# Attention in steps by graph: early masks, one block of weighted sums per graph, keys for two graphs at a time

## The chip, the cores and the metric

The kernel runs on one core of one Trainium2 chip. The metric is device time in microseconds (us), from the first to the last instruction of the core; lower is better. Executions of one kernel agree within 0.3%. A ratio of two kernels is the mean time of one kernel's fast runs over that of the other's of the same rounds on the same chip, so not quite the ratio of the medians that are quoted beside it.

Terms: TensorE does the matrix products and writes them to PSUM, a small memory from which another engine has to copy a result out ("evict" it) before its buffer can be filled again. In profile lines PE is TensorE, PEld its weight loads, DVE VectorE, ACT ScalarE and POOL GpSimd; L191 is line 191 of that run's kernel. The granted clock is the share of full speed at which TensorE was clocked, 1 or 0.5 in these records. A round is the work on four graphs; a run of sums is an unbroken series of weighted sums on TensorE.

## The reference, cut to what matters

128 graphs of 128 nodes with 256 features go through two layers. The first is a graph attention with a feed-forward; the second is an attention in which each of four relations has its own values:

```python
q, k = heads(src @ Wq + bq), heads(src @ Wk + bk)       # 8 heads of 32
attn = softmax(q @ k.T / sqrt(32))
out = 0
for r in range(4):
    v_r = heads(src @ Wv[r] + bv[r])
    out = out + (attn * (adj == r)) @ v_r
x = layernorm(src + out @ Wo + bo)
x = layernorm(x + gelu(x @ W1 + b1) @ W2 + b2)
# cut: the first layer (two graph attentions, layer normalisation, feed-forward)
```

All is float32.

## The kernel before

Four graphs make a group. In each round of the program four stages run on four groups at once: the graph attention (`gat_block`) of one, the first feed-forward (`ff0`) of the one before, the relational attention of the one before that, and the last feed-forward (`ff1`). Each stage is a generator; `together` emits their steps side by side. What is emitted first has priority, and an instruction that is ready may be placed ahead of one that is not, so each engine's fixed order comes from both. The kernel has eight buffers in PSUM: four "mm", two "tr" (transposes), two "av" (weighted sums).

```python
def attention(h, at):
    hT = transposed(h)                 # PE, copies: c=0 by ScalarE, c=1 by VectorE
    for c in range(DC):                # two halves of four heads
        p = mm(wq, hT)
        nc.vector.tensor_scalar(qT[:, c], p, bq.., SCALE, op0=OP.add, op1=OP.mult)
        p = mm(wkk, hT)                # keys of all four graphs
        for q in range(HC):
            nc.scalar.activation(kbd[c][rows, :, q], p[rows], AF.Identity, bias=bk..)
        yield
    ...
    for b in range(G):
        v = values(b)                  # 8 matmuls, evicted by VectorE
        for c in range(DC):
            e = weights(b, c)          # scores, exponential (ScalarE), scaling (GpSimd)
            if pending: by_relation(*pending)   # the half before
            pending = (b, c, e, v, oT)
            yield
    by_relation(*pending)
    layernorm(y, "11")

def by_relation(b, c, e, v, oT):
    # 4 transposes of e into pT, then
    for r in range(R):
        m = wk.tile([P, HC, N], F32, name="m", bufs=4)
        nc.vector.scalar_tensor_tensor(m, ab, r, pT, op0=OP.is_equal, op1=OP.mult)
        for q in range(HC):            # weighted sums on 32 columns of the array
            nc.tensor.matmul(po[ts(q, DH)], v[...], m[:, q], tile_position=(0, q * DH), ...)
    ...                                # copy oT; for the second half: output matmul, add to y

def layernorm(y, k):
    # VectorE: statistics, rstd = var + eps;  GpSimd: rstd ** -0.5
    # VectorE: y = (y - mean) * rstd;         GpSimd: y * gain, y + offset
```

## Time and profile before

| | |
|---|---|
| time, median of 3 | 4056.95 us (4056.15 to 4057.38) |
| TensorE / VectorE / ScalarE / GpSimd busy | 94 / 48 / 35 / 32% |
| mean granted clock of TensorE | 0.975 |
| TensorE idle (span less busy) | 4055.9 - 3807.5 = 248 us |
| TensorE's wait for masks | 82.8 us |
| runs of weighted sums, one relation each mostly | 819 |

The engine that sets the end is TensorE. Its busy share alone is not enough: a change of tile is counted as busy, and a half-speed clock makes busy time longer. So three terms are looked at in all that follows: idle time, time lost to a slow clock (span times one less the mean clock; 4055.9 x 0.025 = 101 us here), and runs of sums. The first two overlap: by the clock records of the trace, 26 of the 101 us fall while TensorE is idle anyway.

### The profile page before, as it was taken

How to read it: one execution, taken by the hardware profiler on the slowest of the kernel's cores; microseconds unless marked ns; L12 is line 12 of the kernel's file. 1: busy time of each engine (PE TensorE's matmuls, PEld its weight loads, DVE VectorE, ACT ScalarE, POOL GpSimd, SP SyncE). 2: the span in 40 equal slices, each digit the busy share in tenths (PEclk: the TensorE clock that was granted, in tenths of full speed). 3: DMA queues.
4: the chain of work that ended last, by engine and by line, in shares of the span. 5: the costliest groups of instructions: out<-in, count | busy, mean ns of one | idle time of the engine just before them, and what ended most of it. 6: DMA issues, size and time to landing. Idle time of an engine off the chain costs nothing.

```text
span 4055.9 us, 50631 instructions
## 1 busy us (share of the span) xinstructions
PE 3807.5 (94%) x19984; PEld 2190.8 (54%) x19984; DVE 1959.5 (48%) x4292; ACT 1439.2 (35%) x4124; POOL 1287.7 (32%) x808
## 2 busy tenths in 40 slices
PE   5799999999999999999999999999999999999997
PEld 4455555555555555555555555555555555555554
DVE  2454554554554544545544545445555455455453
ACT  1233433333333333333333333333343343333332
POOL 1332332333323323323323233233233233233332
PEclk8999999999999999999999999999999999999998
DMA  4000000000000000000000000000000000000000
GB/s 154 6 9 19 19 4 16 19 19 19 19 3 16 19 19 19 3 16 19 19 19 19 4 16 19 19 19 9 14 16 19 19 19 3 11 9 6 6 6 11
DMA packets 28877, 70.75 MB, mean 17 GB/s; under 512 B 5600, under 2 KB 11616, under 8 KB 28640
## 3 DMA queue, kind: packets, MB, share of 16 engines
q1 hardware_dynamic: 21328, 63.19, 4.5%
q10 hardware_dynamic: 7312, 4.34, 0.4%
q8 instruction: 157, 2.57, 0.3%
q14 instruction: 80, 0.66, 0.1%
HBM read 50.74 MB, written 16.78 MB: 17 GB/s over the span
## 4 chain that ended last, share of the span: by engine, by line
PE 75%; POOL 13%; DVE 7%; ACT 1%; issue 1%; DMA 0%; POOLq 0%; DVEq 0%; ACTq 0%
PE mm L201 23%; PE mm L191 18%; PE av L310 8%; PE mm L280 8%; PE mm L288 5%; DVE tok L176 4%; POOL tok L178 3%; POOL tok L179 3%; POOL tok L186 3%; POOL rstd L174 3%; PE tr L303 2%; PE mm L316 2%; PE tr L158 2%; PE mm L263 2%; PE mm L242 1%; PE mm L251 1%
## 5 line engine op out<-in xcount | busy, mean ns | idle before, releaser
L296 POOL TENSOR_TENSOR e<-e,s 128x512 f32<-128x512 f32 x256 | 266.1, 1039 | 1820.9 <-DVE s L295 1691.4
L294 ACT ACTIVATE e<-mm,nm 128x128 f32<-128x128 f32 x1024 | 361.8, 365 | 862.4 <-DVE nm L290 861.3
L308 DVE SCALAR_TENSOR_TENSOR m<-at,tr 128x512 f32<-128x512 int32 x1024 | 645.7, 678 | 4.9 <-PE tr L303 4.9
L191 PE MATMUL mm<-T,w 128*128 128x512 f32 x1024 | 548.4, 651 | 12.5 <-DVE T L160 12.5
L201 PE MATMUL mm<-w,fT 128*128 128x256 f32 x2048 | 515.5, 390 | 0.0
L191 PE MATMUL mm<-T,wf 128*128 128x512 f32 x1024 | 465.1, 602 | 51.8 <-ACT T L162 44.1
L201 PE MATMUL mm<-wf,fT 128*128 128x256 f32 x2048 | 494.9, 387 | 0.0
L310 PE MATMUL av<-m,v 128*32 128x128 f32 x8192 | 414.5, 294 | 85.0 <-DVE m L308 82.8
L280 PE MATMUL mm<-wv,T 128*128 128x512 f32 x1024 | 464.1, 595 | 2.9 <-DVE v L281 2.1
L310 PEld LDWEIGHTS av<-m,v 128*32 128x32 f32 x8192 | 178.7, 112 | 467.9 <-DVE m L308 252.7
L281 DVE TENSOR_TENSOR v<-mm,bv 128x512 f32<-128x512 f32 x256 | 175.7, 687 | 528.8 <-PE mm L280 527.3
L201 PEld LDWEIGHTS mm<-w,fT 128*128 128x128 f32 x2048 | 368.8, 190 | 83.6 <-issue 43.5
L201 PEld LDWEIGHTS mm<-wf,fT 128*128 128x128 f32 x2048 | 373.6, 190 | 74.5 <-issue 25.4
L202 DVE TENSOR_TENSOR tok<-tok,mm 128x512 f32<-128x512 f32 x128 | 88.0, 687 | 655.5 <-PE mm L201 645.0
L178 POOL TENSOR_TENSOR tok<-tok,lng 128x1024 f32<-128x1024 f32 x128 | 300.8, 2350 | 190.2 <-DVE tok L176 190.2
L191 PEld LDWEIGHTS mm<-T,wf 128*128 128x128 f32 x1024 | 188.3, 191 | 273.3 <-issue 178.8
L176 DVE TENSOR_SCALAR tok<-tok,mv,rstd 128x256 f32<-128x256 f32 x512 | 187.0, 430 | 292.4 <-POOL rstd L174 292.4
L280 PEld LDWEIGHTS mm<-wv,T 128*128 128x128 f32 x1024 | 194.8, 191 | 234.9 <-issue 220.3
L179 POOL TENSOR_TENSOR tok<-tok,lnb 128x1024 f32<-128x1024 f32 x128 | 300.8, 2350 | 7.5
L290 DVE TENSOR_REDUCE nm<-mm 128x4 f32<-128x512 f32 x256 | 176.8, 691 | 224.3 <-PE mm L288 224.2
L193 ACT ACTIVATE fT<-mm,b 128x512 f32<-128x512 f32 x256 | 175.9, 687 | 285.1 <-PE mm L191 283.8
L191 PEld LDWEIGHTS mm<-T,w 128*128 128x128 f32 x1024 | 183.0, 199 | 166.3 <-issue 139.6
(65 smaller groups left out, 4402.7 us busy)
## 6 DMA issues: line engine op xcount, KB each, us to landing
xt<-in_xT_dram SPq DMA_DIRECT2D x32, 512.0 KB, 4.4
tok<-in_x_dram SPq DMA_DIRECT2D x32, 512.0 KB, 3.7
out_dram<-tok SPq DMA_DIRECT2D x32, 512.0 KB, 2.6
at<-in_adjT_dram SPq DMA_DIRECT2D x32, 256.0 KB, 2.7
wf<-in_wf_dram SPq DMA_DIRECT2D x2, 1024.0 KB, 9.6
w<-in_w_dram SPq DMA_DIRECT2D x2, 1024.0 KB, 9.6
wv<-in_wv_dram ACTq DMA_DIRECT2D x2, 512.0 KB, 9.9
lng<-in_g_dram ACTq DMA_DIRECT2D x4, 128.0 KB, 6.0
```

Source lines behind the costliest of these rows:

```text
L176: nc.vector.tensor_scalar(y[:, b], y[:, b], mv[:, b, 0:1], rstd[:, b:b + 1], op0=OP.subtract, op1=OP.mult)
L178: nc.gpsimd.tensor_mul(y, y, over_graphs(ln[k][0]))
L179: nc.gpsimd.tensor_add(y, y, over_graphs(ln[k][1]))
L191: nc.tensor.matmul(p, win[:, c, ts(f, P)], hT[:, c], start=c == 0, stop=c == DC - 1)
L201: nc.tensor.matmul(p[:, b - b2_], fT[f][:, ts(b, N)], wout[:, f], start=f == 0, stop=f == FC - 1)
L280: nc.tensor.matmul(p, hT[:, f, ts(b, N)], wv[:, f, r:r + 2], start=f == 0, stop=f == DC - 1)
L288: nc.tensor.matmul(p, qT[:, c, ts(b, N)], kbd[c][:, b], start=True, stop=True)
L290: nc.vector.tensor_reduce(nm, p, AX.X, OP.max, negate=True)
L294: nc.scalar.activation(e[:, q], p[:, q], AF.Exp, bias=nm[:, q:q + 1], accum_out=s[:, q:q + 1])
L296: nc.gpsimd.tensor_mul(e, e, per_row(s, N))
L308: nc.vector.scalar_tensor_tensor(m, ab, r, pT, op0=OP.is_equal, op1=OP.mult)
L310: nc.tensor.matmul(po[ts(q, DH)], v[:, r, c * P + q * DH:c * P + (q + 1) * DH], m[:, q], start=r == 0, stop=r == R - 1, tile_position=(0, ...
```

## The change

The intent: fewer changes of tile, by making all eight masks of a graph first and then all 64 weighted sums in one block; and masks that are ready long before. To make room for eight masks, keys are kept for two graphs, not four.

```diff
+    KG = G // 2
-    kbd = [cst.tile([P, G, HC, N], F32, name=f"kbd{c}") for c in range(DC)]
+    kbd = [cst.tile([P, KG, HC, N], F32, name=f"kbd{c}") for c in range(DC)]
     def attention(h, at):
         hT = transposed(h)
+        yield
         for c in range(DC):
             # cut: the query matmul and its eviction by VectorE stay
-            # cut: keys of four graphs, half c
-            yield
+        def keys(b0):           # cut: keys of graphs b0, b0 + 1, both halves
+        def weights(b):         # cut: both halves; e1 bufs 3 -> 4
+        def by_relation(b, es): # cut: 8 transposes, 8 masks; m bufs 4 -> 8
+        def weighted(ms, v):    # cut: 32 calls = 64 matmuls, one copy of oT
+        keys(0)
+        yield
+        es = weights(0)
+        yield
+        for b in range(G):
+            ms = by_relation(b, es)
+            v = values(b)
+            yield
+            if b + 1 < G:
+                if (b + 1) % KG == 0:
+                    keys(b + 1)
+                es = weights(b + 1)
+                yield
+            oT = weighted(ms, v)
+            yield
+            # cut: output matmul, add to y
         layernorm(y, "11")
-            (attention(...), 10, 0.0, 1.0)
+            (attention(...), 15, 0.0, 1.0)
```

More of the change, by code (lines that the diff above doesn't have):

```diff
@@ L264, in attention @@
             nc.vector.tensor_scalar(qT[:, c], p, bq[:, c:c + 1], SCALE, op0=OP.add, op1=OP.mult)
-            p = ps.tile([P, G, N], F32, name="mm")
-            for f in range(DC):
-                nc.tensor.matmul(p, wkk[:, f, ts(c, P)], hT[:, f], start=f == 0, stop=f == DC - 1)
-            for q in range(HC):
-                rows = ts(q, DH)
-                nc.scalar.activation(kbd[c][rows, :, q], p[rows], AF.Identity, bias=bk[rows, c:c + 1])
-            yield
         y = h
         nc.gpsimd.tensor_add(y, h, over_graphs(bo))
+        def keys(b0):
+            for c in range(DC):
+                p = ps.tile([P, KG, N], F32, name="mm")
+                for f in range(DC):
+                    nc.tensor.matmul(p, wkk[:, f, ts(c, P)], hT[:, f, b0 * N:(b0 + KG) * N],
+                                     start=f == 0, stop=f == DC - 1)
+                for q in range(HC):
+                    rows = ts(q, DH)
+                    nc.scalar.activation(kbd[c][rows, :, q], p[rows], AF.Identity, bias=bk[rows, c:c + 1])
@@ new lines, in weights @@
+        def weights(b):
+            es = []
+            for c in range(DC):
+                p = ps.tile([P, HC, N], F32, name="mm")
+                nc.tensor.matmul(p, qT[:, c, ts(b, N)], kbd[c][:, b % KG], start=True, stop=True)
+                nm = sm.tile([P, HC], F32, name="nm1")
+                nc.vector.tensor_reduce(nm, p, AX.X, OP.max, negate=True)
+                s = sm.tile([P, HC], F32, name="s1")
+                e = wk.tile([P, HC, N], F32, name="e1", bufs=4)
+                for q in range(HC):
+                    nc.scalar.activation(e[:, q], p[:, q], AF.Exp, bias=nm[:, q:q + 1], accum_out=s[:, q:q + 1])
+                nc.vector.reciprocal(s, s)
+                nc.gpsimd.tensor_mul(e, e, per_row(s, N))
+                es.append(e)
+            return es
@@ new lines, in by_relation @@
+        def by_relation(b, es):
+            ab = at[:, b][:, None, :].to_broadcast([P, HC, N])
+            ms = []
+            for e in es:
+                pT = ps.tile([P, HC, N], F32, name="tr", bufs=2)
+                for q in range(HC):
+                    nc.tensor.transpose(pT[:, q], e[:, q], ident)
+                ms.append([])
+                for r in range(R):
+                    m = wk.tile([P, HC, N], F32, name="m", bufs=DC * R)
+                    nc.vector.scalar_tensor_tensor(m, ab, r, pT, op0=OP.is_equal, op1=OP.mult)
+                    ms[-1].append(m)
+            return ms
@@ L283, in values @@
             return v
-        def weights(b, c):
-            p = ps.tile([P, HC, N], F32, name="mm")
-            nc.tensor.matmul(p, qT[:, c, ts(b, N)], kbd[c][:, b], start=True, stop=True)
-            nm = sm.tile([P, HC], F32, name="nm1")
-            nc.vector.tensor_reduce(nm, p, AX.X, OP.max, negate=True)
-            s = sm.tile([P, HC], F32, name="s1")
-            e = wk.tile([P, HC, N], F32, name="e1", bufs=3)
-            for q in range(HC):
-                nc.scalar.activation(e[:, q], p[:, q], AF.Exp, bias=nm[:, q:q + 1], accum_out=s[:, q:q + 1])
-            nc.vector.reciprocal(s, s)
-            nc.gpsimd.tensor_mul(e, e, per_row(s, N))
-            return e
@@ L299, in by_relation @@
-        def by_relation(b, c, e, v, oT):
-            pT = ps.tile([P, HC, N], F32, name="tr", bufs=2)
-            for q in range(HC):
-                nc.tensor.transpose(pT[:, q], e[:, q], ident)
-            po = ps.tile([P, N], F32, name="av", bufs=2)
-            ab = at[:, b][:, None, :].to_broadcast([P, HC, N])
-            for r in range(R):
-                m = wk.tile([P, HC, N], F32, name="m", bufs=4)
-                nc.vector.scalar_tensor_tensor(m, ab, r, pT, op0=OP.is_equal, op1=OP.mult)
-                for q in range(HC):
-                    nc.tensor.matmul(po[ts(q, DH)], v[:, r, c * P + q * DH:c * P + (q + 1) * DH], m[:, q],
-                                     start=r == 0, stop=r == R - 1, tile_position=(0, q * DH))
-            nc.scalar.copy(oT[:, c], po)
-            if c == DC - 1:
-                p = ps.tile([P, D], F32, name="mm")
-                for k in range(DC):
-                    nc.tensor.matmul(p, oT[:, k], wo[:, k], start=k == 0, stop=k == DC - 1)
-                nc.vector.tensor_add(y[:, b], y[:, b], p)
@@ L319, in attention @@
-        pending = None
+        def weighted(ms, v):
+            po = ps.tile([P, DC, N], F32, name="av", bufs=2)
+            for c in range(DC):
+                for r in range(R):
+                    for q in range(HC):
+                        nc.tensor.matmul(po[ts(q, DH), c], v[:, r, c * P + q * DH:c * P + (q + 1) * DH],
+                                         ms[c][r][:, q], start=r == 0, stop=r == R - 1, tile_position=(0, q * DH))
+            oT = wk.tile([P, DC, N], F32, name="oT")
+            nc.scalar.copy(oT, po)
+            return oT
@@ L320, in attention @@
+        keys(0)
+        yield
+        es = weights(0)
+        yield
         for b in range(G):
+            ms = by_relation(b, es)
             v = values(b)
-            oT = wk.tile([P, DC, N], F32, name="oT")
-            for c in range(DC):
-                e = weights(b, c)
-                if pending:
-                    by_relation(*pending)
-                pending = (b, c, e, v, oT)
-                yield
-        by_relation(*pending)
+            yield
[3 more added lines that the diff above has]
+                es = weights(b + 1)
+                yield
+            oT = weighted(ms, v)
+            yield
+            p = ps.tile([P, D], F32, name="mm")
+            for k in range(DC):
+                nc.tensor.matmul(p, oT[:, k], wo[:, k], start=k == 0, stop=k == DC - 1)
+            nc.vector.tensor_add(y[:, b], y[:, b], p)
@@ L365, in graph_layers @@
         got = together(
-            (attention(x1.pop(g2), masks.pop(g2)), 10, 0.0, 1.0) if 0 <= g2 < NG else None,
+            (attention(x1.pop(g2), masks.pop(g2)), 15, 0.0, 1.0) if 0 <= g2 < NG else None,
             (gat_block(*loads.pop(g0)), 5, 0.0, 0.5) if g0 < NG else None,
```

## The prediction

> **What bounds the kernel now.** I read the page first, its busy shares and its slices.
>
> ```profile
> span 4055.9 us, 50631 instructions
> ...
> PE 3807.5 (94%) x19984; PEld 2190.8 (54%) x19984; DVE 1959.5 (48%) x4292; ACT 1439.2 (35%) x4124; POOL 1287.7 (32%) x808
> ...
> PE   5799999999999999999999999999999999999997
> PEclk8999999999999999999999999999999999999998
> ```
>
> TensorE is busy in nine tenths or more of nearly every slice, and no other engine passes half. So the end is set by TensorE's queue: by what it does, and by what holds it. VectorE, ScalarE and GpSimd matter only where TensorE waits for them. A busy TensorE is not one at its peak, so I went on to the timeline of TensorE alone, in an attention step (columns: start, duration in us, engine, line, operation, tiles, count).
>
> ```profile
> 2059.52 1.02 PE L288 MATMUL mm<-kbd,T 128*128 128x512 f32 x2
> 2060.38 0.60 PE L303 MATMUL tr<-ident,e 128*128 128x128 f32 x4
> 2060.82 1.46 PE L201 MATMUL mm<-w,fT 128*128 128x256 f32 x6
> 2062.21 0.42 PE L310 MATMUL av<-m,v 128*32 128x128 f32 x8
> 2062.56 0.70 PE L201 MATMUL mm<-w,fT 128*128 128x256 f32 x2
> 2063.19 0.43 PE L310 MATMUL av<-m,v 128*32 128x128 f32 x8
> 2063.55 0.70 PE L201 MATMUL mm<-w,fT 128*128 128x256 f32 x2
> 2064.18 0.42 PE L310 MATMUL av<-m,v 128*32 128x128 f32 x8
> ```
>
> The reader is to see two things. The weighted sums (L310, tile 128*32) come in runs of 8 instructions, one relation each, because the mask of the next relation (L308) is not there yet and the order was filled with two instructions of the feed-forward. And the times of start: a round of 8 sums and 2 feed-forward instructions takes 2063.19 - 2062.21 = 0.98 us. The same work without the change of tile is cheaper: elsewhere 22 instructions of L201 start within 4.75 us (2054.77 to 2059.52), 0.216 each, so two are 0.43; and a run of 16 sums occupies 0.57 us against 0.355 for a run of 8, so eight more cost 0.215. 0.98 - 0.43 - 0.215 leaves **0.337 us for each excursion into the 32-column tile and back**. Split by the starts, about 0.09 falls on the way in, 0.14 on the way out, 0.10 on the first full instruction after. It is hidden inside "busy" time.
>
> Counting the lines of this timeline over the whole span gives 819 runs of sums: 622 of 8 instructions, 190 of 16, six of 24, one of 32. 819 x 0.337 = 276 us, 6.8% of the span.
>
> The second thing is a wait. TensorE and VectorE in the middle of a round over four graphs (a round repeats every 123.2 us):
>
> ```profile
> 2024.95 1.02 PE L191 MATMUL mm<-T,w 128*128 128x512 f32 x2
> 2028.70 0.43 PE L310 MATMUL av<-m,v 128*32 128x128 f32 x8 [2.73 <-DVE m L308]
> 2029.06 1.40 PE L191 MATMUL mm<-T,w 128*128 128x512 f32 x2
> 2030.38 1.08 PE L310 MATMUL av<-m,v 128*32 128x128 f32 x16
> 2031.40 2.00 PE L191 MATMUL mm<-T,w 128*128 128x512 f32 x2
> ```
>
> ```profile
> 2026.67 1.38 DVE L176 TENSOR_SCALAR tok<-tok,mv,rstd 128x256 f32<-128x256 f32 x4 [2.83 <-POOL rstd L174]
> 2027.96 0.69 DVE L308 SCALAR_TENSOR_TENSOR m<-at,tr 128x512 f32<-128x512 int32 x1
> ```
>
> The mask stands in VectorE's queue behind a layer normalisation that waits for GpSimd; TensorE waits 2.73 us for it. After that its instructions are slow (2.00 us for two of L191, usually 0.86). The table of waits has the total, and the stretch from 2025 to 2050 shows the clock:
>
> ```profile
> PE av L310 <- DVE m L308: 82.8, 35, 2.7
> ...
> 2025.00:2050.00 25.00, 22.27 (x112) 9.41 (x111) 10.92 (x24) 12.57 (x28) 8.38 (x6) 0.93 0.00 1
> ```
>
> A clock of 0.93 over 25 us is 3.4 us at half speed: 1.7 us lost. The stop itself, from start to start, is 2.89 us over the usual pace, so this place costs about 4.6 us a round.
>
> A round adds up: pure streaming by start-to-start paces (0.429 us per 512 columns, 0.216 per 256, 0.109 per transpose, 0.0269 per sum) is 106.9 us; 26 excursions 8.8; the stop and its slow clock 4.6; another stop of 1.55 at the start of the round (L191 waiting for ScalarE's copy of T): 121.9 of 123.2. The remaining 114 us of the span (4056 - 32 x 123.2) are the rounds of filling and emptying.
>
> **What the Trainium skill says.** "TensorEngine Tiling (Array Packing)", Key Properties: "Mode switching requires drain: Changing tiling mode (not just tile) drains the TensorE". The trace agrees: 0.337 us for leaving and re-entering the full array, and nothing between the four column tiles, whose four instructions start within 0.107 us. "TensorE: Matmul & The Clock Gate", Part 1: the clock falls to half after an idle window of about 3.4 us, and the window runs freely. The trace has one half-clock stretch of 3.4 us after most 2.89 us stops, so here a stop shorter than the page's window was enough. The same page, Part 3, The mechanism: matmuls keep strict order, only weight loads move ahead; so one late mask holds everything behind it, as at 2028.70. "ScalarE: Activation LUTs", What ACT_TABLE_LOAD costs: 1283 ns a load; the trace has 187 loads of 1283 ns between exponential and GELU, off the critical path.
>
> **The change part by part.**
>
> *Sums in one block.* The count is unchanged: 2 column halves x 4 relations x 4 heads x 2 instructions = 64 per graph, 128 graphs, 8192. They are emitted after all eight masks, the four value instructions and the next graph's scores. On VectorE the eight masks (8 x about 0.62 us pitch = 5 us) stand ahead of the evictions of the values (2 x 0.69), so when the values are ready all masks are, and nothing forces a break between relations. Perfectly kept, 128 excursions remain: (819 - 128) x 0.337 = **-233 us**, or 22 of 26 excursions, 7.4 us a round.
>
> *Masks early.* Masks of a graph are now emitted two steps before the sums; a step holds some 123/15 = 8 us of TensorE work with the other three stages mixed in. The masks that met the layer normalisation now come either clearly before it (second graph) or have slack (third). The slack is not large: 5 us masks + 1.4 us evictions + 2.9 us behind the normalisation is 9.3 us, against one and a half to two steps. Fully gone: 32 x 4.6 = -147 us. I count somewhat under half, **-65 us**.
>
> *Keys for two graphs.* Matmul columns are equal (twice as many instructions of 256 at 0.216 instead of 512 at 0.429): 0. ScalarE makes 512 evictions of 32x256 instead of 256 of 32x512 at 0.678; from its pace (0.365 at 128 columns, 0.687 at 512) about 0.47 each, 241 against 174: +67 us on an engine at 35%. Keys of graphs 2 and 3 may only be written when the scores of graph 1 are done, and eight evictions (3.8 us) precede the next scores; a step of other work covers that. Allowed: +5 us.
>
> *The rest.* oT is copied 128 times at 256 columns instead of 256 times at 128 (0.264): less ScalarE time, off the path. Exponentials of both halves stand together, so fewer table loads. Both are 0 on the path. Work with larger bursts (transposes holding both "tr" buffers through the masks, values and scores holding all four "mm" buffers) can make new short stops; allowed: +5 us.
>
> Sum: 4057 - 233 - 65 + 5 + 5 = about 3769; I say 3760.
>
> **The rivals.**
>
> *A, the block is split.* The order on TensorE is filled with whatever is ready, so single sums may slip into gaps, as now. For it: 819 runs exist though the source has one block of 32 per half. Against: those breaks lie at missing masks. Two to three runs a graph instead of one give 128 to 256 more excursions, 43 to 86 us: 3800 to 3845.
>
> *B, VectorE's bursts stop TensorE.* Eight masks, two evictions and two maxima are 7.8 us in a row; the evictions of values free PSUM buffers only after it. For it: VectorE's queue already stops TensorE once a round. Against: it is 48% busy. If the stop stays as now: about 3830; with another of that size 3900 to 3950.
>
> *C, everything clears.* The stop and its slow clock go, so does some of the 1.55 us at the start: 4057 - 233 - 147 = 3677, down to 3630.
>
> *D, the switch cost is not the drain.* If TensorE's time were set elsewhere, removing excursions would only lengthen waits: near 4050. Its busy row and the exact repetition of 0.98 us rounds speak against it.
>
> **Range and chances.** The drain saving is well measured, the stop is a coin's throw. Between C nearly whole (3670) and A or B in moderate form (3850) I put 8 chances in 10. Even with the stop kept and the block in two, it is faster by over 5%. Faster by over 2%: 0.94; within 2%: 0.04; slower: 0.02.
>
> **What would show it.** In the timeline of TensorE: runs of 64 sums lasting about 1.8 us, 128 to 200 of them; excursion cost still 0.34. TensorE's matmul count 20240 (256 more for the keys), its busy share still over 90%. In the waits: the sum waiting for a mask falls from 83 us to under 30, and the mid-round half-clock stretches vanish with it. Round time near 114. I am wrong if runs stay at 8 or 16, if a wait for values, for keys or for a PSUM buffer shows some 3 us per round or more, or if the mean clock falls below 0.975.

## More of the kernel before

One place matters later, the start of a round. These are VectorE's, then TensorE's lines of the timeline of the kernel before (start, duration in us, then what it did; in brackets the idle time before and who ended it).

```profile
2075.78 0.75 DVE L264 TENSOR_SCALAR T<-mm,bq 128x512 f32<-128x512 f32 x1 [1.80 <-PE mm L263]
...
2088.88 1.38 DVE L176 TENSOR_SCALAR tok<-tok,mv,rstd 128x256 f32<-128x256 f32 x4 [5.59 <-POOL rstd L174]
2090.18 0.75 DVE L264 TENSOR_SCALAR T<-mm,bq 128x512 f32<-128x512 f32 x1
```

```profile
2087.15 1.88 PE L267 MATMUL mm<-T,wkk 128*128 128x512 f32 x4
2088.87 1.92 PE L233 MATMUL mm<-wx,xt 128*128 128x260 f32 x8
2090.98 3.70 PE L191 MATMUL mm<-T,wf 128*128 128x512 f32 x8 [0.19 <-DVE T L264]
```

VectorE empties the first half of the queries (L264) early, and the second only after a normalisation (L176) that sat 5.59 us waiting for GpSimd. TensorE needs that PSUM buffer for the first feed-forward (L191), and it arrives just in time, 0.19 us late: the key matmuls (L267) and those of the graph attention (L233) fill the gap.

## The result, and the profile after

| | before | after |
|---|---|---|
| time, median of 3 | 4056.95 us | 4122.01 us (4120.36 to 4122.87) |
| ratio, 95% interval | | 1.0161 (1.0141 to 1.0181) |
| runs of weighted sums | 819 | 197 (65 of 64) |
| TensorE idle | 248 us | 4121.1 - 3683.8 = 437 us |
| mean clock; lost to it | 0.975; 101 us | 0.959; 169 us |

The kernel became 1.6% slower: clear of the noise. The page of the changed kernel:

```profile
span 4121.1 us, 51415 instructions
...
PE 3683.8 (89%) x20240; PEld 2349.8 (57%) x20240; DVE 2118.9 (51%) x4292; ACT 1398.2 (34%) x4188; POOL 1287.1 (31%) x808
...
PE   5799889999889898898988898988989889989987
```

TensorE's busy time fell by 124 us and yet the end came later: what was saved came back as idle time, with a slower clock in the busy time that was left. TensorE's timeline shows that the block came out as planned:

```profile
2084.30 7.07 PE L202 MATMUL mm<-w,fT 128*128 128x256 f32 x32
2091.30 1.95 PE L329 MATMUL av<-m,v 128*32 128x128 f32 x64
2093.18 7.17 PE L202 MATMUL mm<-w,fT 128*128 128x256 f32 x32
```

64 sums start within 2093.18 - 2091.30 = 1.88 us, of which 64 x 0.0269 = 1.72 are sums. Over the whole span there are 197 runs where there were 819.

The table of waits of the changed kernel (engine, line, who ended the wait: total us, times, longest) shows what took their place:

```profile
PE mm L192 <- DVE T L266: 146.1, 29, 5.2
...
PE mm L286 <- DVE v L319: 73.7, 29, 2.5
...
PE mm L265 <- DVE T L161: 54.7, 30, 4.2
...
PE mm L243 <- POOL e L223: 28.0, 29, 9.9
PE mm L192 <- DVE tok L353: 26.6, 29, 0.9
PE mm L286 <- ACT kbd L279: 20.1, 63, 0.5
```

The wait for masks (82.8 us before) is gone; in the list of lines 0.5 us of it is left. Four of the six waits are for VectorE. Three of these (L266, L319, L353) do not bring TensorE data that it needs next: the first is a feed-forward matmul "waiting" for a query eviction, with which it shares nothing but a PSUM buffer. They are waits for a buffer to be emptied.

The longest, at the start of a round: TensorE, then VectorE, then the clock in that stretch (columns: stretch, length, busy time of TensorE, its weight loads, VectorE, ScalarE, GpSimd with counts, clock, DMA).

```profile
2110.00 1.89 PE L275 MATMUL mm<-T,wkk 128*128 128x256 f32 x8
2117.09 6.18 PE L192 MATMUL mm<-T,wf 128*128 128x512 f32 x8 [5.21 <-DVE T L266]
```

```profile
2107.45 0.67 DVE L161 COPY T<-tr 128x512 f32<-128x512 f32 x1
...
2112.98 3.40 DVE L177 TENSOR_SCALAR tok<-tok,mv,rstd 128x256 f32<-128x256 f32 x4 [2.82 <-POOL rstd L175]
2116.30 1.40 DVE L266 TENSOR_SCALAR T<-mm,bq 128x512 f32<-128x512 f32 x2
```

```profile
2100.00:2126.00 26.00, 19.09 (x65) 11.40 (x64) 13.65 (x27) 7.77 (x16) 16.03 (x8) 0.87 0.09 33
```

Now both query evictions stand behind the normalisation, which waits for GpSimd and then takes 3.40 us instead of 1.38 (GpSimd's next addition ran beside its first part; why that should matter is not shown). Only half the keys are left to fill the gap (L275: 8 instructions of 256 columns). TensorE stops for 5.21 us, and the eight matmuls after it take 6.18 us, not 3.6: a clock of 0.87 over 26 us is 6.8 us at half speed. The old graphs end earlier in the changed order, too: before, the last masks, sums and addition of a group reached into the next round and the copy of the new hT came ahead of the normalisation; now the normalisation is there first.

In the middle of the round it looks like rival B of the prediction: VectorE makes eight masks in a row and only then empties the values, and the second score matmul (L286) has no buffer. VectorE, then TensorE:

```profile
2058.40 3.39 DVE L177 TENSOR_SCALAR tok<-tok,mv,rstd 128x256 f32<-128x256 f32 x4 [1.12 <-POOL rstd L175]
2061.72 0.41 DVE L353 TENSOR_TENSOR tok<-tok,mm 128x256 f32<-128x256 f32 x1
2062.05 4.86 DVE L309 SCALAR_TENSOR_TENSOR m<-at,tr 128x512 f32<-128x512 int32 x8
...
2066.83 1.28 DVE L319 TENSOR_TENSOR v<-mm,bv 128x512 f32<-128x512 f32 x2
```

```profile
2067.57 2.08 PE L286 MATMUL mm<-kbd,T 128*128 128x512 f32 x2 [2.54 <-DVE v L319]
```

But eight masks alone do not stop TensorE. The wait comes 29 times, once a round, and the same burst comes four times a round. For the round's first graph it reads (VectorE, then TensorE, whose scores start without a wait):

```profile
2004.73 4.87 DVE L309 SCALAR_TENSOR_TENSOR m<-at,tr 128x512 f32<-128x512 int32 x8 [0.47 <-PE tr L305]
2009.53 1.28 DVE L319 TENSOR_TENSOR v<-mm,bv 128x512 f32<-128x512 f32 x2
```

```profile
2011.52 1.88 PE L286 MATMUL mm<-kbd,T 128*128 128x512 f32 x4
```

There the masks start as soon as the transposes are done. In the graph that waits, a normalisation (L177) stands before them and they start at 2062.05, some 6 us after the transposes. So here too a normalisation with its trip to GpSimd comes first, and the burst passes its delay on to the values (values_first and affine_off, below, each take most of this wait away).

The sum of the three terms: runs (819 - 197) x 0.337 = -210 us; idle +189; slow clock +68, of which 22 are counted twice (26 us of the slow clock before and 48 after fall in idle time). Together +25, measured +65; the 40 us left I did not assign.

### The profile page after: what moved, and what is told of

It reads as the page before. It is cut to its first block, busy times and chain, and to the rows that moved or that the text cites. A ratio compares the mean times of both kernels' runs of the same rounds, so it can differ in the third digit from the quotient of the medians.

```text
span 4121.1 us, 51415 instructions
## 1 busy us (share of the span) xinstructions
PE 3683.8 (89%) x20240; PEld 2349.8 (57%) x20240; DVE 2118.9 (51%) x4292; ACT 1398.2 (34%) x4188; POOL 1287.1 (31%) x808
## 4 chain that ended last, share of the span: by engine, by line
PE 62%; DVE 18%; POOL 8%; ACT 7%; issue 2%; POOLq 0%; ACTq 0%; DVEq 0%
PE mm L202 21%; PE mm L192 16%; PE mm L318 8%; DVE tok L177 7%; PE av L329 4%; DVE m L309 4%; PE mm L286 3%; POOL rstd L175 3%; ACT kbd L279 3%; ACT e L292 3%; DVE rstd L174 2%; PE tr L305 2%; PE mm L352 2%; POOL tok L179 2%; POOL tok L180 2%
## 5 line engine op out<-in xcount | busy, mean ns | idle before, releaser
L192 PE MATMUL mm<-T,wf 128*128 128x512 f32 x1024 | 542.5, 679 | 146.1 <-DVE T L266 146.1
L294 POOL TENSOR_TENSOR e<-e,s 128x512 f32<-128x512 f32 x256 | 266.0, 1039 | 832.0 <-DVE s L293 824.9
L192 PE MATMUL mm<-T,w 128*128 128x512 f32 x1024 | 485.6, 613 | 26.6 <-DVE tok L353 26.6
L202 PE MATMUL mm<-wf,fT 128*128 128x256 f32 x2048 | 455.8, 381 | 0.0
L202 PE MATMUL mm<-w,fT 128*128 128x256 f32 x2048 | 455.5, 381 | 0.0
L177 DVE TENSOR_SCALAR tok<-tok,mv,rstd 128x256 f32<-128x256 f32 x512 | 301.8, 651 | 168.1 <-POOL rstd L175 168.1
L286 PE MATMUL mm<-kbd,T 128*128 128x512 f32 x512 | 275.4, 642 | 98.0 <-DVE v L319 73.7
L279 ACT ACTIVATE kbd<-mm,bk 32x256 f32<-32x256 f32 x512 | 238.3, 465 | 284.8 <-PE mm L275 273.5
L268 POOL TENSOR_TENSOR tok<-tok,bo 128x1024 f32<-128x1024 f32 x32 | 75.2, 2350 | 804.1 <-PE tr L159 801.9
L194 ACT ACTIVATE fT<-mm,bf 128x512 f32<-128x512 f32 x256 | 170.8, 702 | 419.3 <-PE mm L192 418.9
L223 POOL TENSOR_TENSOR e<-e,s 128x512 f32<-128x512 f32 x64 | 66.5, 1039 | 777.1 <-DVE s L222 777.1
```

The lines of the kernel that those rows point to most:

```text
L177: nc.vector.tensor_scalar(y[:, b], y[:, b], mv[:, b, 0:1], rstd[:, b:b + 1], op0=OP.subtract, op1=OP.mult)
L192: nc.tensor.matmul(p, win[:, c, ts(f, P)], hT[:, c], start=c == 0, stop=c == DC - 1)
L202: nc.tensor.matmul(p[:, b - b2_], fT[f][:, ts(b, N)], wout[:, f], start=f == 0, stop=f == FC - 1)
L286: nc.tensor.matmul(p, qT[:, c, ts(b, N)], kbd[c][:, b % KG], start=True, stop=True)
L294: nc.gpsimd.tensor_mul(e, e, per_row(s, N))
```

## The experiments

**Theory 1.** The blocks save what was forecast. The loss is waits for PSUM buffers which VectorE, working in order, empties late because a normalisation or eight masks stand in front; each wait is then followed by a slow clock. **Theory 2.** Four "mm" buffers are too few for the new pairs, whoever empties them. **Theory 3.** The blocks save nothing: the price of a change of tile is not on the path. A later rival: the keys for two graphs brought the loss. All kernels gave right results. Cut diffs below leave out lines that only serve the one shown (the scaled bias, buffers).

**q_on_scalar.** The query evictions move from VectorE to ScalarE.

```diff
-            nc.vector.tensor_scalar(qT[:, c], p, bq[:, c:c + 1], SCALE, op0=OP.add, op1=OP.mult)
+            nc.scalar.activation(qT[:, c], p, AF.Identity, bias=bqs[:, c:c + 1], scale=SCALE)
```

> Changed kernel with the two query evictions on ScalarE (bias times scale made once) instead of VectorE. Theory 1: the blocks of sums save some 210 us as forecast, and more than that is given back where VectorE, in order, holds PSUM buffers behind other work; at the start of a round the queries wait behind a layer normalisation (5.2 us for L192, 1.7 us for L265, then half clock). This run takes the 5.2 us wait away: 4122 falls by 150 us of wait and 50 to 80 us of slow clock, to 3890 to 3940. Theory 2: four PSUM buffers are too few wherever they are emptied; the wait moves to another buffer, 4060 to 4120. Theory 3: the blocks of sums save nothing; above 4060 as well.

Measured: 3899.05 us, ratio to before 0.9614 (0.9598 to 0.9631). TensorE's runs of sums are the same 197, and the place now reads (start of a round, TensorE; the feed-forward is L195 here, the keys L278):

```profile
2117.56 1.89 PE L278 MATMUL mm<-T,wkk 128*128 128x256 f32 x8
2119.29 3.60 PE L195 MATMUL mm<-T,wf 128*128 128x512 f32 x8
```

No stop and no slow clock there: idle time fell from 437 to 3897.4 - 3604.8 = 293 us, the clock loss from 169 to 78. One eviction on another engine turned a loss of 1.6% into a gain of 3.9%. Theories 2 and 3 had both expected over 4060.

**values_first.** Values are emitted before the masks.

```diff
-            ms = by_relation(b, es)
             v = values(b)
+            ms = by_relation(b, es)
```

> Changed kernel with the values emitted before the masks of the same graph, so that VectorE empties their two PSUM buffers before the eight masks. Theory 1: only the wait of the scores in the middle of the round goes (L286 for v, 84 us with its slow clock of some 35), 4000 to 4050; the start of the round stays. Theory 2: same direction but under 30 us, since the buffers are refilled at once. Sums may be split into more runs, since the values no longer come last.

Measured: 4021.73 us, 0.9915 (0.9900 to 0.9930): 100 us under the changed kernel, as theory 1 had it. The wait of the scores for values fell from 73.7 to 18.0 us, and the wait for queries stayed at 146.8. But a feed-forward wait for a buffer held by the exponentials came in (45.0 us), so idle time fell by 32 us only; the larger part of the gain is the clock (0.975 instead of 0.959, 56 us less of slow clock in busy time). The runs of sums are 192.

**five_buffers.** A fifth "mm" buffer, one "av" buffer.

```diff
-    ps = ctx.enter_context(tc.tile_pool(name="ps", bufs=4, space=PSUM))
+    ps = ctx.enter_context(tc.tile_pool(name="ps", bufs=5, space=PSUM))
-            po = ps.tile([P, DC, N], F32, name="av", bufs=2)
+            po = ps.tile([P, DC, N], F32, name="av", bufs=1)
```

> Changed kernel with five mm buffers and one av buffer in PSUM[...]. Theory 2 (too few buffers): both waits at PSUM go, 3900 to 3980. Theory 1 (VectorE's order): one more buffer covers 2 to 3 us of each wait of 5.2 and 2.5 us: 4000 to 4060.

Measured: 4043.91 us, 0.9969 (0.9954 to 0.9984). The wait for queries is 98.0 us instead of 146.1 (3.5 each, not 5.2), and the wait for values is now met by a feed-forward matmul (83.6 us). The buffer shortens or moves a wait; it does not remove it. Theory 2's number was missed by 64 us.

**sums_deferred.** The kernel before, with the masks of a half one step ahead of its 32 sums. Keys for two graphs came with it, for memory.

```diff
-                    by_relation(*pending)
+                if masked: sums(*masked)          # condensed; the 32 sums of the half before last
+                if pending: masked = by_relation(*pending)   # transposes and 4 masks
```

> Kernel before, with its own emission order and pace (one half at a time), but the masks of a half are made one step before its 32 sums, eight mask buffers, keys for two graphs to make room. Theory 1: runs of sums fall from 819 to 300 to 450 at 0.34 us each, and the old places of waiting stay: 3870 to 3930. Theory 3 (the switch is not worth its price in the profile): 4030 to 4070.

Measured: 4107.52 us, 1.0125 (1.0110 to 1.0140). A miss: runs fell to 447 as wanted, but the wait for masks rose from 82.8 to 157.2 us. I had taken the keys for harmless in this kernel; the run of keys alone, below, shows that they were not: it took 4186.53 us with the same wait for masks (156.7 us) and 764 runs. Against that fairer control, the 317 runs fewer, 107 us by the price of 0.337, brought 79 us.

**switches_back.** q_on_scalar with a transpose of the identity, which nothing reads, after each relation but a graph's last. The dummy's PSUM buffer is taken from "av", which has one left.

```diff
+                    if (c, r) != (DC - 1, R - 1):
+                        nc.tensor.transpose(dm, ident, ident)
```

> The run with queries on ScalarE (3899 us), plus one transpose of the identity into a bank that nobody reads after each relation's 8 sums but the last of a graph: 896 more changes of tile and back, 896 more transposes of 0.109 us. If an excursion costs 0.337 us on the path: 3899 + 896 x 0.446 = 4299 (4250 to 4320). If the change of tile is hidden by something else (theory 3), only the transposes count: about 4000.

Measured: 4070.25 us, 171 us more than q_on_scalar, well short of 400. The reason is in TensorE's timeline: the dummies depend on nothing, so many stand elsewhere than between two relations, and the runs rose by 776 - 197 = 579, not 896. Where they are in place:

```profile
2010.00 0.43 PE L333 MATMUL av<-m,v 128*32 128x128 f32 x8
2010.36 0.33 PE L336 MATMUL dm<-ident 128*128 128x128 f32 x1
2010.62 0.42 PE L333 MATMUL av<-m,v 128*32 128x128 f32 x8
```

A round of 8 sums and a dummy is 0.616 us; less 0.215 for the sums and 0.109 for the transpose, 0.292 remain per excursion (a change to the 32-column tile and back). 579 x 0.292 + 896 x 0.109 = 267 us more work. The slow clock in TensorE's busy time fell by 20 us (50 to 30), so its busy time should rise by 247 us; it rose by 246. Its idle time fell by 77 us (293 to 216), which leaves 170 us, where 171 were measured. The single "av" buffer cost little: 0.5 us of waits for its copy. Under theory 3 the 98 us of transposes would have been all the added work. So the price per change is real, though the edit put back fewer than intended.

**q_and_values.** Both cures together (the two diffs above).

> Changed kernel with queries on ScalarE and values before masks. Theory 1: the two savings are at different places of the round and add up: 3899 - 100 = 3800 (3775 to 3830). If they were one shortage of buffers that moves about, less than half adds: over 3850.

Measured: 3823.73 us, 0.9431 (0.9415 to 0.9446). The savings nearly add up (223 and 100 alone, 298 together).

**q_values_copies.** In addition, ScalarE copies out both transposed halves.

```diff
-            if c % 2:
-                nc.vector.tensor_copy(t[:, c], p)
-            else:
-                nc.scalar.copy(t[:, c], p)
+            nc.scalar.copy(t[:, c], p)
```

> As the run with queries on ScalarE and values first, and both transposed halves are copied out by ScalarE (before: one each by ScalarE and VectorE). Theory 1: the wait of the query matmuls for VectorE's copy, 55 us, and its slow clock of some 20 go too: 3720 to 3770. Rival: ScalarE's own queue (keys, exponentials, table loads) takes VectorE's place, 3790 or more.

Measured: 3766.89 us, 0.9289 (0.9276 to 0.9303), and the wait of the query matmuls for the copy, 54.9 us in q_and_values, is gone.

**before_q_scalar.** The kernel before with queries on ScalarE.

> Kernel before with the same queries on ScalarE, nothing else. Theory 1: before, TensorE waited only 6 to 17 us for that eviction, so it gains 0 to 30 us: 4025 to 4060. If ScalarE's eviction alone were the reason for 3899, this run would fall by some 150 us too.

Measured: 4091.80 us, 1.0091 (1.0076 to 1.0106): outside the expectation, on the slow side. The runs of sums are the same 819, and the first feed-forward now waits longer for a copy by VectorE (38.9 us instead of 14.4). The cure is no gain by itself; it cures a wait that the change made.

**affine_off.** The changed kernel without gain and offset of the normalisation (one and zero here, so the result stays right on these inputs only).

```diff
-        nc.gpsimd.tensor_mul(y, y, over_graphs(ln[k][0]))
-        nc.gpsimd.tensor_add(y, y, over_graphs(ln[k][1]))
```

> Changed kernel without the multiplication and addition of gain and offset on GpSimd (they are one and zero in these inputs, so the result stays right here, though not in general). Theory 1: the normalisation on VectorE then finds its rstd at once, the queries behind it are not held, the waits of 5.2 and 1.7 us at the start of the round and part of the 2.5 us in the middle go with their slow clock: 3830 to 3950. Rival: VectorE's sheer amount of work, not its wait for GpSimd, holds the buffers: 4060 to 4120.

Measured: 3845.89 us, 0.9480 (0.9466 to 0.9494). GpSimd free at once, TensorE's wait for query evictions disappears from the table of waits (146 us before), and that of the scores for values falls to 7.8 us. The wait for the copy of hT doubled (111.4 us); the order changed too. So GpSimd's work, not the number of VectorE's instructions, which is the same, held the queue. How much of that is the trip for rstd and how much the slowing of VectorE beside GpSimd the run does not part: the normalisation's own time on VectorE (L177) fell as well, from 301.8 to 241.3 us.

**keys_alone.** The kernel before with keys for two graphs.

> Kernel before with one part of the change alone: keys for two graphs, made twice a round. Theory 1: ScalarE's extra evictions are not on the path, 4040 to 4085. Rival (the keys brought the loss): 4110 or more, with TensorE waiting for kbd by 50 us or more.

Measured: 4186.53 us, 1.0315 (1.0298 to 1.0332). The time matches the rival, but by another way than it named: TensorE does not wait for keys, but for masks (156.7 us, before 82.8). In the middle of a round TensorE now reads:

```profile
2083.92 1.03 PE L264 MATMUL mm<-T,wkk 128*128 128x256 f32 x4
2088.96 1.85 PE L316 MATMUL av<-m,v 128*32 128x128 f32 x24 [4.01 <-DVE m L314]
```

Before, scores, output and feed-forward stood ahead of this sum; the scores now need new keys and come after it, so TensorE reaches the missing mask earlier and waits 4.01 us instead of 2.73. Some 30 such stops make about half of the 74 us; short waits for single masks make the rest, and the feed-forward's waits for VectorE's copy of T grew from 14.4 to 63.5 us.

**best_five_buffers** and **best_norm_later.** q_values_copies with the fifth buffer, and with attention's normalisation emitted in the next round.

```diff
-        layernorm(y, "11")          # at the end of attention
+            (norm11(x2.pop(g3)), 1, NL, 0.5)   # NL = 0.25: a stage of its own, a round later
```

> The run with queries and copies on ScalarE and values first (3767 us), with five mm buffers and one av buffer. Theory 1: what is left there are waits for buffers held by the exponentials (45 us) and for values (20 us); one more buffer covers these: 3700 to 3745. Rival: the single av buffer makes the sums of the next graph wait for its copy, 3770 or more.

> The run with queries and copies on ScalarE and values first (3767 us), with attention's layer normalisation emitted a quarter of a round later, in the next round. Theory 1: at the round's start nothing waits for it any more, so little moves: 3740 to 3780. If it falls under 3720, normalisations still cost where no wait for them is shown.

Measured: 3799.94 us, 0.9367 (0.9353 to 0.9381), and 3776.75 us, 0.9310 (0.9296 to 0.9324). Five buffers are worse: with one "av" buffer the output matmul waits for the copy of the sums, 66.5 us in all. Moving the normalisation gains nothing there (3777 against 3767 us), which fits that no urgent eviction stands behind it any more.

The loss of keys_alone left a question: do the two side parts of the change, new first steps and keys for two, cost as much inside the changed kernel? Five runs answer it.

**start_as_before** and **start_look.** The changed kernel with the old first steps.

```diff
         hT = transposed(h)
-        yield
         for c in range(DC):
             # cut: query half c
+            keys(0, (c,))       # cut: keys(0) after the loop goes
+            if c == 0:
+                yield
```

> Changed kernel with the first two steps of an attention as before (transposes, queries and keys of the first half; then of the second), the rest as changed. If those steps caused the wait at the round's start, it goes: 3890 to 4000. If the earlier end of the old graphs' sums did (it lets both normalisations into VectorE's queue ahead of the new round), the wait for the query eviction stays at 100 us or more: 4060 to 4150.

> The same kernel as start_as_before, for a profile: its fast time was 4042. If the first steps shorten the wait of L192 for the query eviction, that wait is 60 to 90 us in total instead of 146; the slow clock falls with it.

Measured: 4042.33 us, 0.9968 (0.9952 to 0.9985). One execution, the one profiled, took 13187 us; it is left out as slow, and the second look (a single run, so of unknown state, but at 4039.09 us like the fast ones) gives the profile. The time fell between the two alternatives: the wait for the query eviction is 79.9 us, about half of 146.1. So the first steps are part of the cause, not all.

**two_keys_small** and **four_keys_small.** The changed kernel with a few buffers less (three e1, one cap, one oT, three small), with keys for two and for four graphs.

```diff
-    KG = G // 2
+    KG = G
```

> Control for the next run: changed kernel with three e1 buffers, one cap, one oT and three small buffers, to save memory; keys still for two graphs. Expected near the changed kernel, 4100 to 4180.

> The same with keys for four graphs, as before the change: the keys part undone in the changed kernel. If keys cost on the path there (the scores wait for kbd 17 to 41 us in the profile), it is 20 to 60 us under the control. If they cost as much as in the run of keys alone, about 130 us under it. If nothing, within 15 us.

Measured: 4117.18 us (1.0154) and 3980.06 us (0.9817; 0.9803 to 0.9832). The saving of buffers does nothing; the keys cost 137 us. Little of it is a wait for keys (11.9 us in the control). With all keys at the round's start there are 3.4 us of matmuls (L275) to bridge the wait there instead of 1.7, so the wait is 3.5 us each, not 5.2 (98.3 against 144.5 us in all):

```profile
2035.57 3.60 PE L275 MATMUL mm<-T,wkk 128*128 128x512 f32 x8
2042.67 3.70 PE L192 MATMUL mm<-T,wf 128*128 128x512 f32 x8 [3.51 <-DVE T L266]
```

That is 46 of the 77 us by which idle time fell (429 to 352). The middle of the round loses two waits and gains one (the scores for values 73.7 to 20.4, a buffer behind L353 26.8 to none, a copy of T 67.6 new); why, no run takes apart. The runs fall from 197 to 164 and the clock rises from 0.957 to 0.970. The control also shows that the change need not have halved the keys: room for eight masks was to be had from buffers that cost nothing.

**blocks_alone.** Old first steps and old keys; of the change only paired halves, early masks and blocks are left.

> Changed kernel with first steps and keys both as before (memory saved as in the control): what is left of the change is the pairing of halves, the early masks and the blocks of sums. Theory: without the two side parts the blocks' saving is seen: 3860 to 3960. If the loss lies in the blocks' own emission, 3980 or more.

Measured: 3921.30 us, 0.9668 (0.9651 to 0.9684). The start of its round, TensorE:

```profile
2013.88 1.88 PE L265 MATMUL mm<-T,wkk 128*128 128x512 f32 x4
2016.48 3.67 PE L192 MATMUL mm<-T,wf 128*128 128x512 f32 x8 [0.72 <-DVE T L276]
```

So the four combinations are, in medians:

| | new first steps | old first steps |
|---|---|---|
| keys for two | 4122 | 4042 |
| keys for four | 3980 | 3921 |

Keys cost 121 to 142 us, first steps 59 to 80, together 201 us, and the rest of the change gains 134 us on the kernel before. (The lower row has the smaller buffers, which cost nothing measurable.)

**best_four_keys.** q_values_copies with keys for four graphs.

> The run with queries and copies on ScalarE and values first (3767 us), with keys for four graphs and the memory saved as in the control. There no wait at the round's start is left to bridge, so less than in the changed kernel: 3700 to 3760. If keys for two cost by themselves (more instructions, ScalarE's evictions), 3640 to 3690.

Measured: 3728.12 us, 0.9192 (0.9178 to 0.9206), 8.1% under the kernel before and the best of all. Its page:

```profile
span 3725.3 us, 50467 instructions
...
PE 3531.2 (95%) x19984; PEld 2266.1 (61%) x19984; DVE 2095.6 (56%) x4133; ACT 1402.8 (38%) x4092; POOL 1293.4 (35%) x808
```

TensorE idle is down to 194 us, at a clock of 0.990; the work of VectorE is still 56%, but no long wait hangs on it. Here the keys are worth 39 us (3767 to 3728), not 137, which fits that most of their worth in the changed kernel was in waits that are gone here.

## Why the prediction was wrong, by its own steps

- **What bounds the kernel: right.** TensorE's queue, by what it does and what holds it.
- **"Sums in one block", -233 us: right.** 128 to 200 runs were forecast, 197 came: -210 us. switches_back bears out a price of 0.29 us, and blocks_alone the direction. (The 0.98 us in its sum is 0.985 in the trace; with the printed digits 0.335 would come out, not 0.337.)
- **"Masks early", -65 us: right as far as it goes, and too narrow.** The wait for masks fell to 0.5 us. But the half-clock stretches did not vanish with it, because the same delay of VectorE reached TensorE by another way, as a wait for the values' PSUM buffers (73.7 us). The prediction reckoned that the masks would come clear of the normalisation or have slack; in one graph a round they still stood behind it. This is near rival B, which I had priced at 3900 to 3950 in all and given too little weight; but the burst of masks that B names is not enough, as the other graphs of the round show.
- **"Keys for two graphs", "Allowed: +5 us": wrong, the largest failed term.** It cost 137 us (four_keys_small). "A step of other work covers that" looked at the key evictions alone, and those are indeed nearly covered. What was overlooked is that the key matmuls themselves were the work that covered something else, the wait at the start of the round: 46 us of idle time by the measurement. For the waits in the middle of the round that came and went with the keys the cause stays open.
- **"The rest", "Allowed: +5 us": wrong.** The new first steps cost 59 to 80 us. The start of the round had been in view only as a stop of 1.55 us; that the second query eviction stood behind a normalisation that waited 5.59 us for GpSimd, with 0.19 us to spare on TensorE, could have been read from VectorE's timeline.
- **The sum of these.** -233 and -65 met +10 allowed, where the side parts alone cost 201 us. The blocks without them gain 134 us, which is short of 298 as well: in blocks_alone 655 runs fewer are 221 us, but idle time is 31 us longer than before (waits for copies of T, 67.5 and 62.7 us, are new or longer) and the slow clock in busy time 30 us; the 26 us left are not assigned. The floor was too high as well: "faster by over 5%" with the stop kept and the block in two does not follow from the prediction's own 3830 and 43 us, which make 4.5%.
- **The signs named for being wrong came true:** a wait for a PSUM buffer of 3 us a round or more (5.0 us), and a mean clock under 0.975 (0.959). TensorE's busy share is 89%, not over 90%.

Not settled: why VectorE's normalisation took 3.40 us beside GpSimd (62 of the 512 instructions of L177 took over 1 us, 5 before the change), and how much of each wait is the earlier end of the old graphs and how much the order within the first steps.

## What to carry to other kernels

When a change moves or removes work on the busiest engine, ask what that work was covering: walk through the start and the end of a round on every engine that empties its PSUM buffers, and note each wait that is met with less than a microsecond to spare. A buffer comes free only when everything ahead of its eviction in that engine's queue is done, as with the 5.21 us here; so evictions that the busy engine needs soon belong on a queue without long trips to a third engine. And test the parts of a change one by one: here the main part gained 3.3%, two side parts cost 5%, and with one of these undone, two kinds of eviction moved to another engine and one emission moved, the whole was worth 8.1%. The cures overlap: several of them, each alone, turn the loss into a gain, and their worths alone do not simply add.

## What the Trainium skill lacked or had wrong

- "TensorEngine Tiling (Array Packing)", Key Properties, names the drain at a change of tiling mode but gives no price: here 0.337 us for going to four column tiles and back between matmuls of 256 columns, 0.292 us around a single transpose, and 276 us of 4056 in the kernel before.
- "TensorE: Matmul & The Clock Gate", Part 1, puts the fall to half clock after an idle window of about 3.4 us. Here shorter stops were enough, but not always: by the clock records all 30 stops of some 2.7 us of the kernel before were followed by half clock, and 14 of the 29 stops of 2.54 us after the change. Most such stretches last 3.41 or 6.83 us.
- No page that I read says that the PSUM buffer a matmul waits for can be held by the order of another engine's queue, behind an eviction that has nothing to do with it: 146 us of waits of the first feed-forward for queries in the changed kernel, where a fifth buffer brought 78 us and another queue 223.
